# A graph layer on one core: a drain behind every second gather, and 36 instead of 24 groups whose rows all come from TensorE

## The chip, the cores and the metric

The program runs on one core of one Trainium2 chip. The metric is the device time in microseconds of one execution; for the kernel before there are three runs, and one more execution was taken by the hardware profiler. Engines are named as in the profile: PE is TensorE's matmul, PEld its weight load, DVE VectorE, ACT ScalarE, POOL GpSimd, SP SyncE.

## The reference

One layer of a graph network with 6250 nodes of 64 features and 206250 edges, sorted by their target `dst`:

```python
h = jnp.maximum(_layernorm(x, axis=-1), 0.0)
msg = jax.nn.relu(h[src] + edge_attr)
agg = jax.ops.segment_sum(msg, dst, num_segments=x.shape[0])
h = jax.nn.relu((h + agg) @ W1 + b1)
x = x + (h @ W2 + b2)
```

Two steps are hard here: fetching the row `h[src]` for each of the 206250 edges, and summing the messages by target.

## The kernel before, in words

**Groups and sets.** The edges are cut into 268 groups of 768 edges (128 partitions by 6 columns) and a smaller tail group. Groups 0 to 4 are handled in the prologue. The other 264 are bound into 144 *sets* (`GROUPS`, L61 to L63): most sets are two groups, 24 are a single group. Eleven groups make six sets, of which the second is single; six sets make two *chunks* of three.

**Two ways to fetch a row.** For a pair of groups, columns 0 to 2 of each come by GpSimd: one indirect DMA per column (`gather`, L226; the instruction is L229) takes 128 rows of 256 bytes out of `h_rows` in HBM into a slot of the ring `xg`. Columns 3 to 5 come from TensorE. A single group has no gather (`WHOLE`, `pool_cols`, L238): all six of its columns come from TensorE. So each set has six columns of 128 rows from TensorE, and a pair has six gathers besides.

**TensorE's way.** h stands in SBUF as two float16 parts (`hp`). A counting sort, three sets to a chunk and some ten sets ahead (`rank_at` to `sourced`, L327 to L416), gives each edge a place. Then, for two sets at a time, one-hot matrices made by DVE (`found` L564, `backs` L574) select rows by matmul: `across_of` (L586; 8 matmuls L594 at a time) selects, ACT copies the result (L599), `turn_of` (L601; 4 matmuls L604) transposes, ACT copies again (L612), and `pick` (L614; the matmuls L618) puts the rows in the order of the edges. `decode_parts` and `decode_sum` (L683, L684, L690) put the two parts together.

**Messages and sums.** `decode` (L692) adds the picked rows to the edge attributes (DVE, L698, twice a set), and for a pair the gathered rows (DVE, L701, once). ACT takes the relu (`messages`, L708). `window_sum` (L718) sums the messages of a group by 6 matmuls with a one-hot matrix (L722; the one-hot is L655), and DVE adds the window into z (L645). Blocks of 512 nodes that are complete go through the two layers (L748, L758) and out.

**What sets the order.** The order on each engine is that in which the code records the instructions; nothing reorders them. `both_units` (L883) records set k: in each of three steps a turn, an across and two picks, with the decoding of set k-1, the messages and window sums of set k-2 and the counting for sets ahead between them. GpSimd gets its gathers nine sets ahead (`AHEAD`, ring of 11 slots): five times in a set, `pick` calls `fetch_next` (L263), which records one gather of the list `pending` with a manual dependency on the pick's matmul: the gather may start only when that matmul is done. In the prologue the gathers of groups 0 to 20 are recorded in long rows (L1021 to L1034), partly behind matmuls or DVE instructions. DVE's only use of a gathered row is L701. SP issues all other loads.

```python
HEAD = 2 * RG - 1
for g in range(F0, NG + 1, HEAD):
    GROUPS += [(g, g + 1), (g + 2,), (g + 3, g + 4), (g + 5, g + 6), (g + 7, g + 8), (g + 9, g + 10)]
```

`places` (L293) prepares the search for a range of chunks on DVE, in small steps that `searching` (L841) records twice in a set; `stretches` (L284) cuts the columns for it by the pattern of the sets, and `rank_fits` (L366) does so for the slots.

Of the kernel before, what the change touches and what calls it, by code (L numbers as in the profile page):

```python
# [21 lines left out]
G = 6  # L22
GE = P * G
NG = E // GE
# [17 lines left out]
H = 3  # L42
# [13 lines left out]
F0 = 5  # L56
SETS = 3
RG = 2 * SETS
HEAD = 2 * RG - 1
assert (NG + 1 - F0) % HEAD == 0 and SETS == 3  # L60
GROUPS = []  # L61
for g in range(F0, NG + 1, HEAD):
    GROUPS += [(g, g + 1), (g + 2,), (g + 3, g + 4), (g + 5, g + 6), (g + 7, g + 8), (g + 9, g + 10)]  # L63
KS = len(GROUPS)
KD = KS // 2
WHOLE = [gs[0] for gs in GROUPS if len(gs) == 1]
NCH = KS // SETS
# [4 lines left out]
RING, AHEAD, EAS = 11, 9, 4  # L72
# [8 lines left out]
def kernel(  # L81
# [14 lines left out]
    nc = tc.nc  # L96
# [110 lines left out]
    def rows_of(g):  # L207
        if g >= F0:
            return ring(xgs, g)
        if g not in raws:  # L210
            raws[g] = lnp.tile([P, G, D], F32, name="xr", bufs=F0)
        return raws[g]
# [10 lines left out]
    beats, paces = [], []  # L223
    beat = mybir.DependencyInfo(mybir.DependencyClass.Sync, mybir.DependencyReason.ANTI)

    def gather(xg, idx, n, rows, behind=()):  # L226

        for j in range(n):
            it = nc.gpsimd.indirect_dma_start(  # L229
                out=xg[:, j, :], out_offset=None, in_=rows[:, :],  # L230
                in_offset=bass.IndirectOffsetOnAxis(ap=idx[:, j:j + 1], axis=0))
            if j >= n - len(behind):
                tc.add_manual_dep(it.ins, behind[j - n + len(behind)].ins.name, beat, reason="pace")

    def first_col(g):
        return 0 if g < NG else G - CT

    def pool_cols(g):  # L238
        return G if g < F0 else 0 if g in WHOLE else G - H

    def fetch(g, behind=()):
        lo, hi = first_col(g), pool_cols(g)
        if hi:
            gather(rows_of(g)[:, lo:], src_sb[:, g * G + lo:g * G + hi], hi - lo, x if g < RAW else h_rows, behind[lo:])
# [5 lines left out]
    def attr_set(k):  # L250
        gs = GROUPS[k]
        if len(gs) == 2 and gs[1] < NG:
            g = gs[0]
            nc.sync.dma_start(out=eas[(k + RAWS) % EAS].rearrange("p g j d -> p g (j d)"),
                              in_=edge_attr[g * GE:(g + 2) * GE, :].rearrange("(g p j) d -> p g (j d)", g=2, j=G))
        else:
            for g in gs:
                attr_load(ring(eas, g), g)

    pending = [(g, j) for k in range(AHEAD, KS) for g in GROUPS[k] for j in range(first_col(g), pool_cols(g))]  # L260
    assert all(5 * (set_of[g][0] - RING + 1) <= n for n, (g, j) in enumerate(pending))

    def fetch_next(behind):  # L263
        if pending:
            g, j = pending.pop(0)
            gather(rows_of(g)[:, j:], src_sb[:, g * G + j:], 1, h_rows, [behind])

# [15 lines left out]

    def stretches(t_sb, c0, c1):  # L284

        g0 = F0 + c0 // 2 * HEAD
        t = t_sb[:, g0 * G:(g0 + (c1 - c0) // 2 * HEAD) * G].rearrange("p (e g j) -> p e g j", g=HEAD, j=G)
        return ((t[:, :, :2, G - H:], 0, slice(0, 2)),
                (t[:, :, 2:3].rearrange("p e o (g j) -> p e (o g) j", j=H), 0, slice(2, 4)),
                (t[:, :, 3:RG - 1, G - H:], 0, slice(4, RG)),  # L290
                (t[:, :, RG - 1:, G - H:], 1, slice(0, RG)))

    def places(c0, c1):  # L293
        n = c1 - c0
        held = [work.tile([P, WB], F32, name="ow").bitcast(I16) for _ in range(2)]

        def at(i):
            return held[i // 3][:, i % 3 * n * CC:][:, :n * CC].rearrange("p (c s) -> p c s", s=CC)

        own, off, row, second, third = at(0), at(1), at(3), at(4), at(5).bitcast(F16)  # L300
        for src, w, gs in stretches(src_sb, c0, c1):
            nc.vector.tensor_copy(own.rearrange("p c s -> p (c s)")
                                  .rearrange("p (e w g j) -> p e w g j", w=2, g=RG, j=H)[:, :, w, gs], src)
            yield
        nc.vector.tensor_scalar(row, own, 1.0 / RR, 0.5 / RR + 0.5, op0=ALU.mult, op1=ALU.add)
        yield
        nc.vector.scalar_tensor_tensor(off, row, float(-RR), own, op0=ALU.mult, op1=ALU.add)
        yield
        it = nc.vector.tensor_scalar(second, off, 1.0 / PARTS, (RR + 0.5) / PARTS - 0.5, op0=ALU.mult, op1=ALU.add)
        if c0 == 2:  # L310
            paces.append(it)
        yield
        nc.vector.scalar_tensor_tensor(node[:, c0:c1], second, float(PP), row, op0=ALU.mult, op1=ALU.add)
        yield
        nc.vector.tensor_scalar(third, second, float(BB), quarter[:, 0:1], op0=ALU.is_equal, op1=ALU.mult)
        yield
        nc.vector.scalar_tensor_tensor(off, second, float(-PARTS), off, op0=ALU.mult, op1=ALU.add)
        yield
        it = nc.vector.scalar_tensor_tensor(part[:, c0:c1], off, float(RR + BIAS // STEP), third, op0=ALU.add, op1=ALU.add)
        if c0 == 2:  # L320
            paces.append(it)
# [43 lines left out]

    def rank_fits(c):  # L366
        rk = ranks.pop(c).rearrange("p (g j) -> p g j", j=H)
        pieces = ((0, 2, G - H), (2, 4, 0), (4, RG, G - H)) if c % 2 == 0 else ((0, RG, G - H),)
        for u, to, c0 in pieces:
            g = GROUPS[c * SETS + u // 2][0]  # L370
            if c0:
                mine = slot[:, g * G:(g + to - u) * G].rearrange("p (g j) -> p g j", j=G)[:, :, c0:]
            else:
                mine = slot[:, g * G:(g + 1) * G].rearrange("p (g j) -> p g j", j=H)
            nc.vector.scalar_tensor_tensor(mine, rk[:, u:to], float(AMONG + S), mine, op0=ALU.is_lt, op1=ALU.mult)
            yield
# [237 lines left out]
    def pick(k, i, t):  # L614
        d, u = k // 2, k % 2 * 2 + i
        ps = pick_banks[k % 2][i][:, :2 * H * D].rearrange("p (w t d) -> p w t d", w=2, t=H)
        for q in range(Q):
            it = nc.tensor.matmul(ps[:, :, t], backs[d][:, q % QW, q // QW, u * H + t, :],  # L618
                                  picked[d][:, q, u].rearrange("p (w d) -> p w d", w=2), start=(q == 0), stop=(q == Q - 1))
            if (u * H + t) % 2 == q // QW and q % QW == QW - 1 and (u * H + t) % (2 * H) < 2 * H - 1:  # L620
                fetch_next(it)

    def norm_edges(xg):
        s = work.tile([P, G], F32, name="raw_s")
# [183 lines left out]
    searches = []  # L808
# [32 lines left out]
    def searching(u):  # L841
        for c, to in zip(PLACED[2:], PLACED[3:]):
            if u == max(0, 2 * RG * (c // 2) - 60):
                searches.append(places(c, to))
        if searches and next(searches[0], True):
            searches.pop(0)

    def across_at(a):
        if a < KD * Q:
# [31 lines left out]
    behind = []  # L881

    def both_units(k):  # L883
# [11 lines left out]
        for s in range(3):  # L895
# [22 lines left out]
            for t in range(2):  # L918
                pick(k, *divmod(2 * s + t, H))
# [38 lines left out]
    for _ in places(0, 2):  # L958
        pass
# [153 lines left out]
    wide = hot.tile([P, PARTS * BB + J, 4, S], F16, name="found").rearrange("p m u s -> p (m u s)").bitcast(F32)[:, :WB]  # L1113
    with tc.If(any_left > 0):
# [18 lines left out]
        for c in range(NB + 1):  # L1133
            o, xb = result(c, *hidden(c))
# [41 lines left out]
```

## Time and profile before

| what | value |
|---|---|
| median of three runs | 1317.23 us (1314.55 to 1322.07) |
| the profiled execution | 1329.39 us |
| its span, first to last instruction | 1327.7 us |
| mean granted TensorE clock | 0.918 |
| gathers (xg; prologue's xr) | 718; 18 + 12 |
| matmuls | 15593 |
| DMA | 173.72 MB, 131 GB/s on the mean |

Of the page's 40 slices these are the rows of the granted TensorE clock and of the DMA engines' busy share, both in tenths:

```profile
PEclk9767988989999999899998998989889999999898
DMA  5222444444444444444444444444444444444441
```

The first three slices are the prologue, then one steady stage runs to the end. The last gather is issued at 1267.4 us, so in the last 60 us GpSimd has next to nothing to do. A group's row, as they follow in the prediction, reads: line, engine, operation, output and inputs, shapes, count; then busy time in us, mean ns of one; then the idle time of the engine just before them and what ended most of it. "issue" means that the profile shows nothing that was waited for.

### The profile page before, as it was taken

The numbers are of one execution on the slowest core, as the hardware profiler recorded it, in microseconds if no ns is written. First come the engines' busy times: TensorE is split into PE (matmuls) and PEld (weight loads), VectorE is DVE, ScalarE is ACT, GpSimd is POOL, SyncE is SP. The second block draws the span as 40 slices with busy tenths as digits, with TensorE's granted clock in tenths as the row PEclk, the third lists the DMA queues.
The fourth block names the chain that finished last, engine by engine and source line by source line (L and its number), as shares of the span: only waits on it lengthen the run. The fifth ranks groups of instructions, "written<-read, shape, count | busy, mean of one in ns | idle before, by whom it ended". The sixth has DMA issues, their size and how long they took to land. (4 is left out here: it accounts for less than half of the span.)

```text
span 1327.7 us, 39109 instructions
## 1 busy us (share of the span) xinstructions
PE 1041.3 (78%) x15593; PEld 925.0 (70%) x15593; DVE 855.2 (64%) x2167; ACT 853.0 (64%) x1849; POOL 764.3 (58%) x763
## 2 busy tenths in 40 slices
PE   0235888878887887888888888888888887888897
PEld 0224777777776777777777777777777776777796
DVE  8672766666576676576566665665666765766684
ACT  3334666666666666666666666666666666666685
POOL 7674665655565665565565565655566666566510
PEclk9767988989999999899998998989889999999898
DMA  5222444444444444444444444444444444444441
GB/s 187 81 60 93 141 134 128 144 134 122 144 138 135 146 139 134 142 119 134 130 139 140 137 138 127 138 129 139 137 139 141 139 138 141 138 139 141 127 127 55
DMA packets 92790, 173.72 MB, mean 131 GB/s; under 512 B 23673, under 2 KB 61178, under 8 KB 92602
## 3 DMA queue, kind: packets, MB, share of 16 engines
q1 hardware_dynamic: 68554, 146.58, 33.4%
q0 software_dynamic: 23936, 24.56, 9.3%
q8 instruction: 124, 2.03, 0.6%
q14 instruction: 64, 0.52, 0.2%
q10 hardware_dynamic: 112, 0.03, 0.0%
HBM read 167.22 MB, written 3.87 MB: 129 GB/s over the span
## 5 line engine op out<-in xcount | busy, mean ns | idle before, releaser
L229 POOL DMA_INDIRECT xg<-h_rows,src_sb x718 | 730.9, 1018 | 494.1 <-PE pick L618 209.3
L618 PE MATMUL pick<-picked,backs 128*128 128x128 f16 x5184 | 412.2, 230 | 35.3 <-issue 33.8
L618 PEld LDWEIGHTS <-backs 128*128 128x128 f16 x5184 | 329.8, 103 | 61.1 <-issue 50.3
L612 ACT CAST picked<-half 128x512 f16<-128x512 f32 x432 | 249.1, 577 | 177.8 <-remote 53.2
L698 DVE SCALAR_TENSOR_TENSOR ea<-pick,ea 128x192 f32<-128x192 f32 x288 | 101.7, 354 | 401.6 <-PE pick L722 108.1
L599 ACT CAST across<-half 128x512 f16<-128x512 f32 x432 | 253.7, 587 | 158.7 <-PE pick L618 57.4
L594 PE MATMUL half<-found,hp 128*128 128x128 f16 x3456 | 288.4, 229 | 22.9 <-issue 19.9
L594 PEld LDWEIGHTS <-hp 128*128 128x128 f16 x3456 | 233.8, 103 | 39.5 <-issue 31.0
L574 DVE TENSOR_SCALAR backs<-spots,ids 128x1536 f16<-128x1536 int16 x432 | 255.2, 637 | 0.0
L722 PE MATMUL pick<-oh,ea 128*64 128x32 f32 x3176 | 143.2, 226 | 82.1 <-issue 60.2
L722 PEld LDWEIGHTS pick<-oh,ea 128*64 128x64 f32 x3176 | 117.8, 138 | 118.3 <-issue 88.1
L604 PE MATMUL half<-ident_h,across 128*128 128x128 f16 x1728 | 179.4, 229 | 18.0 <-ACT across L599 13.7
L683 ACT CAST both<-pick 128x384 f16<-128x384 f32 x288 | 140.1, 486 | 62.9 <-issue 17.6
L564 DVE TENSOR_SCALAR found<-sources,nodes_of 128x1536 f16<-128x1536 int16 x288 | 170.3, 638 | 9.7 <-issue 9.7
L604 PEld LDWEIGHTS <-across 128*128 128x128 f16 x1728 | 131.0, 103 | 27.2 <-ACT across L599 14.4
L708 ACT ACTIVATE ea<-ea 128x768 f32<-128x768 f32 x144 | 114.5, 795 | 0.7 <-DVE ea L701 0.7
L684 ACT ACTIVATE minus<-both 128x192 f16<-128x192 f16 x288 | 104.5, 363 | 9.1
L655 DVE TENSOR_TENSOR oh<-slot,pick 128x384 f32<-128x384 int16 x144 | 74.0, 514 | 0.3 <-PE pick L690 0.3
L690 PE MATMUL pick<-both,weigh_high 128*128 128x192 f16 x288 | 72.6, 252 | 0.2 <-ACT both L683 0.2
L690 PE MATMUL pick<-minus,weigh_sign 128*128 128x192 f16 x288 | 72.3, 251 | 0.4 <-issue 0.3
L690 PE MATMUL pick<-both,ident_h 128*128 128x192 f16 x288 | 72.5, 252 | 0.0
L690 PE MATMUL pick<-minus,weigh_last 128*128 128x192 f16 x288 | 72.0, 250 | 0.0
(135 smaller groups left out, 809.1 us busy)
## 6 DMA issues: line engine op xcount, KB each, us to landing
sources<-source_row SPq DMA_DIRECT2D x72, 768.0 KB
ea<-in_edge_attr_dram SPq DMA_DIRECT2D x118, 384.0 KB
spots<-spot_rows SPq DMA_DIRECT2D x72, 384.0 KB
xg<-h_rows,src_sb POOLq DMA_INDIRECT x718
ea<-in_edge_attr_dram SPq DMA_DIRECT2D x32, 192.0 KB
xb<-in_x_dram SPq DMA_DIRECT2D x12, 128.0 KB
out_dram<-o SPq DMA_DIRECT2D x12, 128.0 KB
h_rows<-x SPq DMA_DIRECT2D x3, 384.0 KB
```

What stands on the lines that cost most here:

```text
L229: it = nc.gpsimd.indirect_dma_start(out=xg[:, j, :], out_offset=None, in_=rows[:, :], in_offset=bass.IndirectOffsetOnAxis(ap=idx[:, j:j + ...
L564: nc.vector.tensor_scalar(found[d][:, b * PARTS + m:b * PARTS + m + PARTS // 2].rearrange("p m u s -> p (m u s)"), sources[d][:, m * 4 * S ...
L574: nc.vector.tensor_scalar(backs[d][:, q, w].rearrange("p t s -> p (t s)"), spots[d].bitcast(I16), ids[:, w * QW + q:w * QW + q + 1], None, ...
L594: last = nc.tensor.matmul(ps[:, j * P:(j + 1) * P], hp[:, b * PARTS + m].rearrange("p t d -> p (t d)"), found[d][:, b * PARTS + m].rearran ...
L599: nc.scalar.copy(across[d, q].rearrange("p u j s -> p j u s"), ps.rearrange("p (j u s) -> p j u s", j=J, u=4))
L604: last = nc.tensor.matmul(ps[:, u * P:(u + 1) * P], ac[:, u].rearrange("p j s -> p (j s)"), ident_h, start=True, stop=True)
L612: nc.scalar.copy(picked[d][:, q].rearrange("p u d -> p (u d)"), turned.pop((d, q)))
L618: it = nc.tensor.matmul(ps[:, :, t], backs[d][:, q % QW, q // QW, u * H + t, :], picked[d][:, q, u].rearrange("p (w d) -> p w d", w=2), st ...
L683: nc.scalar.copy(both[:, i], picks_of(k, i))
L690: nc.tensor.matmul(picks_of(k, i)[:, 0], weights, rows, start=(j == 0), stop=(j == len(terms) - 1))
L708: nc.scalar.activation(msg, msg, AF.Relu)
L722: last = nc.tensor.matmul(pa[i * D:(i + 1) * D], msg[:, j, :], oh[:, j, :], start=(j < lo + 2), stop=(j >= G - 2))
```

## The change

Two things are changed, and three places follow them.

First, `gather` counts its gathers, and behind every second one it records a drain of GpSimd, an instruction of that engine which has no operands and moves no data. That holds for the prologue's gathers as well.

Second, the pattern of the sets: the first 33 groups keep it (three times six sets with one single set). The other 231 are bound in eleven times twelve sets of 21 groups: six sets as before, then six with two single sets. That makes 150 sets (75 pairs of sets, 50 chunks) of 144, 36 single ones, and 114 pairs with 682 gathers.

What follows: `fetch_next` gets the number of the set and issues at four of its five calls for the sets that lie in a six with two single ones (`RATES`, `gates`); `stretches`, `places` and `rank_fits` know the new pattern; and `searching` records two steps instead of one in its first twelve calls.

```diff
+HEAD, PAIR = 2 * RG - 1, 4 * RG - 3
+SINGLES, DOUBLES = 3, 11
+for h in range(SINGLES + 2 * DOUBLES):
+    last = h >= SINGLES and (h - SINGLES) % 2
+    GROUPS += [(g, g + 1), (g + 2,), (g + 3, g + 4)]
+    g += 5
+    GROUPS += [(g, g + 1), (g + 2,), (g + 3, g + 4)] if last else [(g, g + 1), (g + 2, g + 3), (g + 4, g + 5)]
+    g += 5 if last else 6
+    RATES += [4 if last else 5] * 2 * SETS
...
+            gathers[0] += 1
+            if gathers[0] % 2 == 0:
+                nc.gpsimd.drain()
...
-    def fetch_next(behind):
-        if pending:
+    def fetch_next(k, behind):
+        rate = RATES[min(k + AHEAD, KS - 1)]
+        gates[0] += rate
+        if pending and gates[0] >= 5 * (gates[1] + 1):
+            gates[1] += 1
+            assert k < set_of[pending[0][0]][0] < k + RING
             g, j = pending.pop(0)
             gather(rows_of(g)[:, j:], src_sb[:, g * G + j:], 1, h_rows, [behind])
...
-        pieces = ((0, 2, G - H), (2, 4, 0), (4, RG, G - H)) if c % 2 == 0 else ((0, RG, G - H),)
+        pieces = ((0, 2, G - H), (2, 4, 0), (4, RG, G - H)) if len(GROUPS[c * SETS + 1]) == 1 else ((0, RG, G - H),)
...
-                fetch_next(it)
+                fetch_next(k, it)
...
-        if searches and next(searches[0], True):
-            searches.pop(0)
+        for _ in range(2 if u < 2 * RG else 1):
+            if searches and next(searches[0], True):
+                searches.pop(0)
```

How it moves instructions shows first on DVE, at the decoding of the 41st set, the second of the new single sets. Before (`ea` are the edge attributes, `xg` the gathered rows, `pick` the picked ones, `oh` the one-hot of the window sums):

```order
L574 TENSOR_SCALAR backs<-spots,ids 128x1536
L698 SCALAR_TENSOR_TENSOR ea_145<-pick_195,ea_145 128x192
L698 SCALAR_TENSOR_TENSOR ea_145<-pick_196,ea_145 128x192
L701 SCALAR_TENSOR_TENSOR ea_145<-xg_156,ea_145 128x2x192
L655 TENSOR_TENSOR oh<-slot,pick_195 128x384
L645 ISA
L645 TENSOR_TENSOR z<-z,pick_195 128x32
```

and now:

```order
L600 TENSOR_SCALAR backs<-spots,ids 128x1536
L724 SCALAR_TENSOR_TENSOR ea_145<-pick_204,ea_145 128x192
L724 SCALAR_TENSOR_TENSOR ea_145<-pick_205,ea_145 128x192
L681 TENSOR_TENSOR oh<-slot,pick_204 128x192
L671 ISA
L671 TENSOR_TENSOR z<-z,pick_204 128x32
```

The set has lost its use of gathered rows, and its one-hot is that of one group.

On GpSimd the gathers are listed one ring slot after another, six to a pair of groups (`xg` numbered by the ring of eleven slots; `src_sb` holds the row numbers, `h_rows` is the table in HBM). The drains are not listed in this view. Before, around the 29th set, the first of the new single ones, whose slot is 155:

```order
L229 DMA xg_150<-h_rows,src_sb 128x64 x6
L229 DMA xg_151<-h_rows,src_sb 128x64 x6
L229 DMA xg_153<-h_rows,src_sb 128x64 x6
L229 DMA xg_154<-h_rows,src_sb 128x64 x6
L229 DMA xg_155<-h_rows,src_sb 128x64 x6
L229 DMA xg_156<-h_rows,src_sb 128x64 x6
L229 DMA xg_146<-h_rows,src_sb 128x64 x6
L229 DMA xg_148<-h_rows,src_sb 128x64 x6
```

and now:

```order
L238 DMA xg_150<-h_rows,src_sb 128x64 x6
L238 DMA xg_151<-h_rows,src_sb 128x64 x6
L238 DMA xg_153<-h_rows,src_sb 128x64 x6
L238 DMA xg_154<-h_rows,src_sb 128x64 x6
L238 DMA xg_156<-h_rows,src_sb 128x64 x6
L238 DMA xg_146<-h_rows,src_sb 128x64 x6
L238 DMA xg_148<-h_rows,src_sb 128x64 x6
```

The six gathers into slot 155 are gone; in each row of six that is left, three drains stand, behind the second, fourth and sixth gather. On TensorE the list grows from 24,494 to 25,500 rows, which is 503 weight loads and 503 matmuls more.

More of the change, by code (lines that the diff above doesn't have):

```diff
@@ L58 @@
 RG = 2 * SETS
[L59 to L63, printed above, removed]
+HEAD, PAIR = 2 * RG - 1, 4 * RG - 3
+SINGLES, DOUBLES = 3, 11
+assert F0 + SINGLES * HEAD + DOUBLES * PAIR == NG + 1 and SETS == 3
+GROUPS, RATES = [], []
+g = F0
+for h in range(SINGLES + 2 * DOUBLES):
[5 more added lines that the diff above has]
+    RATES += [4 if last else 5] * 2 * SETS
 KS = len(GROUPS)
@@ L224 @@
     beat = mybir.DependencyInfo(mybir.DependencyClass.Sync, mybir.DependencyReason.ANTI)
+    gathers = [0]
     def gather(xg, idx, n, rows, behind=()):
@@ L260 @@
     pending = [(g, j) for k in range(AHEAD, KS) for g in GROUPS[k] for j in range(first_col(g), pool_cols(g))]
-    assert all(5 * (set_of[g][0] - RING + 1) <= n for n, (g, j) in enumerate(pending))
-    def fetch_next(behind):
-        if pending:
+    gates = [0, 0]
+    def fetch_next(k, behind):
[4 more added lines that the diff above has]
+            assert k < set_of[pending[0][0]][0] < k + RING
             g, j = pending.pop(0)
@@ L284, in stretches @@
     def stretches(t_sb, c0, c1):
[L286 to L291, printed above, removed]
+        wide = c0 >= 2 * SINGLES
+        n, size, chunks = ((c1 - c0) // 4, PAIR, 4) if wide else ((c1 - c0) // 2, HEAD, 2)
+        assert n * chunks == c1 - c0 and (wide or c1 <= 2 * SINGLES)
+        g0 = GROUPS[c0 * SETS][0]
+        t = t_sb[:, g0 * G:(g0 + n * size) * G].rearrange("p (e g j) -> p e g j", g=size, j=G)
+        parts = []
+        for w in range(chunks):
+            a = GROUPS[(c0 + w) * SETS][0] - g0
+            if len(GROUPS[(c0 + w) * SETS + 1]) == 1:
+                parts += [(t[:, :, a:a + 2, G - H:], w, slice(0, 2)),
+                          (t[:, :, a + 2:a + 3].rearrange("p e o (g j) -> p e (o g) j", j=H), w, slice(2, 4)),
+                          (t[:, :, a + 3:a + 5, G - H:], w, slice(4, RG))]
+            else:
+                parts += [(t[:, :, a:a + RG, G - H:], w, slice(0, RG))]
+        return chunks, parts
     def places(c0, c1):
@@ L300, in places @@
         own, off, row, second, third = at(0), at(1), at(3), at(4), at(5).bitcast(F16)
-        for src, w, gs in stretches(src_sb, c0, c1):
+        chunks, parts = stretches(src_sb, c0, c1)
+        for src, w, gs in parts:
             nc.vector.tensor_copy(own.rearrange("p c s -> p (c s)")
-                                  .rearrange("p (e w g j) -> p e w g j", w=2, g=RG, j=H)[:, :, w, gs], src)
+                                  .rearrange("p (e w g j) -> p e w g j", w=chunks, g=RG, j=H)[:, :, w, gs], src)
             yield
```

## The prediction

> **What bounds the kernel now.** I read the busy shares first, then the windows of the stages, then what TensorE and GpSimd waited for, and last the timeline of a few microseconds. The busy shares settle nothing:
>
> ```profile
> PE 1041.3 (78%) x15593; PEld 925.0 (70%) x15593; DVE 855.2 (64%) x2167; ACT 853.0 (64%) x1849; POOL 764.3 (58%) x763
> ```
>
> Nobody is full, TensorE (PE) least idle. The windows say more. The first of these two is the steady stage, the second begins just after the last gather; the columns are PE, weight loads, DVE, ACT, POOL, then the granted clock, DMA share and GB/s.
>
> ```profile
> core 0: us, PE busy (x) PEld busy (x) DVE busy (x) ACT busy (x) POOL busy (x), PEclk, DMA share, GB/s
> 200.00:1200.00 1000.00, 834.74 (x12638) 745.24 (x12639) 649.17 (x1641) 669.34 (x1470) 594.30 (x587) 0.94 0.45 136
> 1268.00:1289.00 21.00, 21.00 (x388) 20.23 (x385) 17.08 (x43) 19.71 (x42) 0.34 (x1) 1.00 0.42 137
> ```
>
> In the steady stage TensorE does 12638/1000 = 12.6 matmuls per us. In the 21 us without gathers it does 388/21 = 18.5, with no idle time and the full clock, at the same 137 GB/s. The sets there still run all their picks, turns and window sums. So a set is not limited by what TensorE computes but by something that ends when the gathers end. At 18.5 per us the 12638 matmuls would have taken 684 us; the other 316 us, over 587 gathers, are **0.54 us lost per gather**.
>
> How it happens is seen in one burst. First GpSimd's timeline, then TensorE's (start, duration, line, in brackets the idle time before it):
>
> ```profile
> 630.77 0.94 POOL L229 DMA_INDIRECT xg<-h_rows,src_sb  x1 [0.30 <-PE pick L690]
> 632.02 0.94 POOL L229 DMA_INDIRECT xg<-h_rows,src_sb  x1 [0.30 <-issue]
> 633.27 0.94 POOL L229 DMA_INDIRECT xg<-h_rows,src_sb  x1 [0.30 <-issue]
> 634.51 0.94 POOL L229 DMA_INDIRECT xg<-h_rows,src_sb  x1 [0.30 <-issue]
> 637.61 1.03 POOL L229 DMA_INDIRECT xg<-h_rows,src_sb  x1 [2.15 <-PE pick L618]
> ```
> ```profile
> 633.45 0.65 PE L722 MATMUL pick<-oh,ea 128*64 128x32 f32 x15 [0.44 <-issue]
> 635.01 0.32 PE L722 MATMUL pick<-oh,ea 128*64 128x32 f32 x4 [0.53 <-issue]
> 636.47 0.43 PE L722 MATMUL pick<-oh,ea 128*64 128x32 f32 x3 [0.54 <-issue]
> 636.83 1.46 PE L618 MATMUL pick<-picked,backs 128*128 128x128 f16 x12
> 1276.03 0.89 PE L722 MATMUL pick<-oh,ea 128*64 128x32 f32 x24
> ```
>
> Gathers stand 0.30 us apart from 630.77 to 635.45. The 24 window sums (L722) begin in it and need from 633.45 to 636.8, against 0.89 us in the last row, where no gather runs. TensorE waits for nothing that the profile names ("issue"), and is released about 1 us after the burst. The prologue has a longer case:
>
> ```profile
> 94.00:101.00 7.00, 3.06 (x27) 2.40 (x25) 6.38 (x16) 1.26 (x3) 5.17 (x7) 0.50 0.48 128
> 101.00:113.00 12.00, 0.16 (x2) 0.00 (x0) 0.00 (x0) 0.00 (x0) 7.15 (x8) 0.50 0.36 127
> ```
>
> For 12 us only GpSimd works there. Joined gathers seem to be what hurts. How many are joined, and how large TensorE's unnamed waits are, stands in the list of waits for 200 to 1200 us:
>
> ```profile
> POOL xg L229 <- PE pick L618: 176.7, 173, 2.8
> POOL xg L229 <- issue: 66.7, 214, 1.7
> PE pick L722 <- issue: 53.1, 97, 1.2
> PE pick L618 <- issue: 29.7, 83, 1.2
> ```
>
> 214 of 587 gathers follow another after 66.7/214 = 0.31 us.
>
> **The change part by part.** The regrouping makes 150 sets of 144. The window sums stay, since the groups stay 268; each new set brings its picks, halves, turns and decoding:
>
> ```profile
> L618 PE MATMUL pick<-picked,backs 128*128 128x128 f16 x5184 | 412.2, 230 | 35.3 <-issue 33.8
> L594 PE MATMUL half<-found,hp 128*128 128x128 f16 x3456 | 288.4, 229 | 22.9 <-issue 19.9
> L604 PE MATMUL half<-ident_h,across 128*128 128x128 f16 x1728 | 179.4, 229 | 18.0 <-ACT across L599 13.7
> L690 PE MATMUL pick<-both,weigh_high 128*128 128x192 f16 x288 | 72.6, 252 | 0.2 <-ACT both L683 0.2
> ```
>
> Over 144 sets these are 36, 24, 12 and, the last row being one of four alike, 8 per set; with half an L589 and two more chunks of 10 counting matmuls that is 6 x 80.5 + 2 x 10 = 503 matmuls. At the pace without gathers they cost 503/18.5 = **+27 us**; at the pace with gathers 503/12.6 = 40 us. I take the first, because the gathers are priced by themselves: 718 become 682, 36 x 0.54 = **-19 us**. These two parts alone are worth +8 us.
>
> ACT gets six sets' copies, DVE six sets' compares and some 18 more casts of the search for places, by these rows 18 x 0.2 us:
>
> ```profile
> L302 DVE CAST ow<-src_sb 128x48 int16<-128x48 int32 (+3 forms) x8 | 1.7, 215 | 0.3 <-issue 0.3
> L612 ACT CAST picked<-half 128x512 f16<-128x512 f32 x432 | 249.1, 577 | 177.8 <-remote 53.2
> ```
>
> Both engines have a third of the steady stage free, so I price that at nothing; ACT is 19.71 of 21 us busy without gathers, so if the pace came near 18.5 matmuls per us, ACT would be next. SP issues three more pairs of source and spot loads, at a DMA share of 0.45, for nothing. The paced gathers fall from 5 a set to 4 in eleven of the 25 chunk pairs; they are issued nine sets ahead, so a late one has some 70 us before DVE adds it (L701).
>
> **The drain.** 341 of them stand behind gathers of xg (and 15 in the prologue behind others). Behind each, the next gather's wait and the gather are queued, and only DVE's L701, nine sets later, waits for those. The trace has no drain after a gather; nearest are GpSimd's own drains, the first after memsets, the others at the program's end:
>
> ```profile
> L1162 POOLq DRAIN  x1: 188/188/188, 0.4 to 0.4; - x1
> L1171 POOLq DRAIN  x3: 40/107/9212, 1301.0 to 1327.4; - x3
> ```
>
> So the duration lies between 0.04 and 9.2 us. I take 0.19 us: it is the drain behind work of GpSimd's own, and the gather's record has ended before it. Can GpSimd afford it? A gather takes
>
> ```profile
> L229 POOL DMA_INDIRECT xg<-h_rows,src_sb x718 | 730.9, 1018 | 494.1 <-PE pick L618 209.3
> 1151.08 3.33 DMA xg<-h_rows,src_sb
> ```
>
> 1.02 us and about 0.30 to the next, so a pair 2.64. Of the 682, 42 are issued in the prologue (14 groups of three), 640 are paced. The picks, which pace the gathers, run now from 120.5 to 1314.3 us:
>
> ```profile
> L618 PE MATMUL pick<-picked,backs x5184: 216/219/314, 120.5 to 1314.3; 128*128 128x128 f16 x200
> ```
>
> If these 1194 us become 1140 (the sum below), a pair has 1140/320 = 3.56 us, and the drain is covered up to **0.9 us**; beyond, GpSimd sets the pace.
>
> What the drain may gain is the loss of the joined gathers. At least nothing; at most everything that gathers cost, 640 x 0.54 = 346 us. Between: 214/587 = 36% of the gathers are joined, a drain behind every second gather stands in half of the joints, 18% of 640 = 117 gathers, and each gets a pause ahead of it in which TensorE can be released. At the mean price that is 117 x 0.54 = **-63 us**. It rests on the burst above, where the release comes after the run of gathers and not within it. The stand of 12 us in the prologue may shrink as well; I count nothing for it.
>
> The sum, on the profiled execution's own 1329.4 us (its span is 1327.7): 1329.4 + 27 - 19 - 63 = 1274 us. The median of the runs shown is 1317.2, 0.991 of the profiled one, so I predict 1274 x 0.991 = **1262 us**.
>
> The clock is part of it: 0.94 in the steady stage, 1.00 without gathers, 0.50 in the prologue's stand. By the Trainium skill (TensorE: Matmul & The Clock Gate, The HAM clock gate) the clock is halved after a window of about 3.4 us in which TensorE is idle; the rows agree in that the slow clock stands where TensorE stood still. By it the clock's share comes back with the stalls and is no further term.
>
> **The rivals.**
>
> *The drain changes nothing for TensorE.* The regrouping remains: 1329.4 + 8 = 1337, or 1325 us. For it: within the burst the drain's 0.19 us is short beside the 1 us that TensorE needs to be released. Against it: where a gather waited for a pick, the pause was 176.7/173 = 1.02 us on the mean, and there TensorE runs.
>
> *The pace without gathers is an accident of the program's end.* Then gathers hold nobody, the new sets cost the mean pace and the 36 gathers give nothing back: 1329.4 + 40 = 1369, or 1357 us, slower. For it: the counting of ranks has ended by 1268 us too. Against it: that is 20 of about 640 matmuls in six sets, while the pace rises by half, and DMA stays at 137 GB/s. The Trainium skill (SBUF — State Buffer, SBUF: two separate sides) says that TensorE's ports never wait on anyone and that only GpSimd and VectorE share one, which speaks for this rival: by it no gather could hold TensorE. The burst and the 12 us do not agree with that, though no row names what is held.
>
> *The drain itself holds TensorE, or GpSimd becomes the bound: slower.* A us of gather costs 0.54/1.02 = 0.53 us. If a drain costs in the same proportion and frees nothing, 341 x 0.19 x 0.53 = 34 us are added: 1371, or 1359 us. If a drain lasts longer than the 0.9 us of cover, GpSimd decides: at 1.2 us a pair takes 3.84, 320 pairs 1229 us where 1194 stood, so 1329 - 1194 + 1229 = 1364 or 1352 us; if it waits for the landing, 3.33 us in the row above, a pair takes 5.97, and 1329 - 1194 + 1910 = 2045, or 2027 us. For it: the 9.2 us drain at the end. Against it: that one follows other instructions of the program's end, 30 us after the last gather. The Trainium skill (PSUM — Partial Sum Buffer, Engine vs sequencer instructions) says that a drain waits for the engine to go fully idle; whether a transfer counts as the engine's, no run here shows.
>
> *More than I count comes back.* If the pauses end half of what gathers cost, 173 us, the sum is 1164, or 1154 us. A long burst is worse than its share, by the prologue; against it, a drain behind every second gather cuts only one or two of the three joints of a burst of four.
>
> **How the numbers follow.** My forecast, with a gain between a third and twice of the 63 us (1305 to 1200), has a chance of 0.50. More than that 0.10. No effect of the drain, 1306 to 1335 us, 0.14. The accident 0.09. The drain as a cost or a bound, 1340 us and more, 0.17. Ten in a hundred lie below 1200, and of the slow cases those of a GpSimd bound, some eight, above 1360: the range is 1200 to 1360; the forecast's own is 1200 to 1305. What a measurement can tell from no change is about 0.5%, so 1310.6 to 1323.8 us: half of the no-effect case and a little of the forecast's edge, 0.09. Faster is 0.50 + 0.10 and a little of the no-effect case, 0.61; slower the rest, 0.30.
>
> **What would show it.** Right: in 200 to 1200 us over 13.3 matmuls per us, fewer gathers that follow another after 0.30 us, "issue" before L722 clearly under 53 us in 1000, the granted clock over 0.94, the drains around 0.2 to 0.6 us and DVE's L701 never waiting for a transfer. The matmuls grow by 503, the xg gathers are 682. Wrong in the drain's gain: the pace at 12.6 with these waits as they are. Wrong in its cost: GpSimd's idle time before a gather ended by nothing but issue, DVE waiting for xg. Wrong in the regrouping's price: no change of the pace, and the end 40 us later. The accident is refuted if the stage behind the last gather again runs at over 18 matmuls per us while the steady pace changes.

## The result, and the profile after

The changed program takes 1824.5 us (median of four, 1819.2 to 1831.5), the program before beside it 1319.7: a ratio of 1.380 with the interval 1.375 to 1.386. The prediction of 1262 us has the wrong sign, and the time lies 465 us above its range.

The windows of the same stretch as before (PE, weight loads, DVE, ACT, POOL, the granted clock, DMA share, GB/s) show every engine less busy, GpSimd too:

```profile
200.00:1200.00 1000.00, 653.14 (x9202) 597.95 (x9200) 476.34 (x1227) 494.26 (x1079) 396.12 (x398) 0.82 0.33 98
```

9.2 matmuls per us instead of 12.6, and 0.40 gathers per us instead of 0.59. Nobody is full because somebody waits, and the list of waits of 200 to 1700 us (total us, times, longest) says for what:

```profile
DVE ea L727 <- DMA xg<-h_rows,src_sb: 649.8, 100, 12.0
ACT picked L638 <- PE half L630: 535.4, 141, 9.6
PEld L644 <- issue: 482.9, 109, 9.1
PE pick L644 <- DVE z L671: 466.2, 91, 9.0
POOL xg L238 <- issue: 261.9, 287, 4.8
```

DVE waits 6.5 us at a time for gathered rows (L727, which was L701). Behind it in DVE's order stands the sum into z (L671), for that waits TensorE, and for TensorE ACT. So one late thing starts the chain: the gathers, which are ordered nine sets ahead. The lines of the drain (duration min/median/max in ns, first and last start), of the gathers and of the picks show the length of the chain:

```profile
L243 POOLq DRAIN  x356: 3126/3690/10583, 3.5 to 1802.1; - x178
L238 POOL DMA_INDIRECT xg<-h_rows,src_sb x682: 942/946/4747, 83.9 to 1803.0; - x171
L644 PE MATMUL pick<-picked,backs x5400: 216/219/314, 117.0 to 1802.8; 128*128 128x128 f16 x193
```

A drain lasts 3.69 us at the median, not 0.19, and the gathers now go on to the last microsecond; before, they ended some 60 us ahead. Three pieces of one cycle show what a drain is made of: GpSimd's timeline, one drain by itself, and the chain of waits at that place.

```profile
640.96 0.99 POOL L238 DMA_INDIRECT xg<-h_rows,src_sb  x1 [2.40 <-DVE ea L727]
642.25 0.95 POOL L238 DMA_INDIRECT xg<-h_rows,src_sb  x1 [0.30 <-issue]
645.54 0.95 POOL L238 DMA_INDIRECT xg<-h_rows,src_sb  x1 [2.34 <-PE pick L644]
```
```profile
L243 POOLq DRAIN  x1: 3496/3496/3496, 636.7 to 636.7; - x1
```
```profile
637.62 2.43 DMA xg<-h_rows,src_sb
640.05 0.03 issue
640.08 0.05 DVEq L727
640.13 0.04 issue
640.18 0.13 DVE ea L727
```

The second gather of the pair begins at 637.62 and its rows have landed at 640.05. The drain began at 636.67, beside the first gather, and lasted 3.50 us: it ends at 640.17, 0.12 us after the landing. So it is with each of the 335 drains after 120 us: from the landing to the drain's end 0.11 to 0.12 us, while the drains themselves differ between 3.1 and 7.2 us. A drain here waits until the rows are there. The next gather begins 0.79 us later, at 640.96; the releasers named in its brackets, DVE and TensorE, are only the last semaphores that were set meanwhile. By the Trainium skill (Perfetto Trace Analysis, DMA Instruction — SWDGE (GPSIMD)) the record of such a gather ends when its descriptors are written and not when the data has moved; the rows agree, with a record of 0.95 us and a landing 2.4 us after its start.

The cycle of a pair adds up: 0.31 us from the first gather to the drain's start, 3.95 the drain on the mean, 0.77 from its end to the next gather, 5.03 in all; 335 pairs are 1685 us, and from the first pick to the last gather are 1803.0 - 117.0 = 1686. GpSimd's chain fills the whole time.

### The profile page after: what moved, and what is told of

It is laid out like the page before. It is cut to its first block, busy times and chain, and to the rows that moved or that the text cites. A ratio compares the mean times of both kernels' runs of the same rounds, so it can differ in the third digit from the quotient of the medians.

```text
span 1818.4 us, 40621 instructions
## 1 busy us (share of the span) xinstructions
PE 1147.5 (63%) x16096; PEld 1045.2 (57%) x16096; DVE 883.1 (49%) x2266; ACT 890.3 (49%) x1923; POOL 716.1 (39%) x727
## 4 chain that ended last, share of the span: by engine, by line
issue 21%; PE 17%; POOLq 10%; POOL 10%; DMA 7%; DVE 2%; DVEq 1%; ACT 0%; ACTq 0%
POOLq L243 10%; POOL xg L238 10%; DMA xg<-h_rows,src_sb 7%; PE pick L644 7%; PE half L620 3%; PE pick L716 2%; PE half L630 2%; PE pick L748 1%; DVE oh L681 1%; DVEq L565 1%; PE half L615 1%; DVE ea L727 0%; PE rows L774 0%; PE rows L784 0%; DVE z L671 0%
## 5 line engine op out<-in xcount | busy, mean ns | idle before, releaser
L238 POOL DMA_INDIRECT xg<-h_rows,src_sb x682 | 682.6, 1001 | 1039.8 <-issue 334.3
L644 PE MATMUL pick<-picked,backs 128*128 128x128 f16 x5400 | 459.6, 245 | 514.4 <-DVE z L671 512.3
L644 PEld LDWEIGHTS <-backs 128*128 128x128 f16 x5400 | 390.2, 111 | 540.8 <-issue 530.8
L727 DVE SCALAR_TENSOR_TENSOR ea<-xg,ea 128x384 f32<-128x384 f32 x114 | 63.6, 558 | 714.3 <-DMA xg<-h_rows,src_sb 714.3
L620 PE MATMUL half<-found,hp 128*128 128x128 f16 x3600 | 312.7, 236 | 2.5 <-issue 1.1
L620 PEld LDWEIGHTS <-hp 128*128 128x128 f16 x3600 | 258.8, 108 | 22.3 <-issue 17.2
L630 PE MATMUL half<-ident_h,across 128*128 128x128 f16 x1800 | 198.5, 239 | 1.5 <-ACT across L625 0.9
L630 PEld LDWEIGHTS <-across 128*128 128x128 f16 x1800 | 148.4, 109 | 5.7 <-ACT across L625 1.4
L748 PE MATMUL pick<-oh,ea 128*64 128x32 f32 x3176 | 123.9, 226 | 6.6 <-ACT ea L734 6.4
L716 PE MATMUL pick<-both,weigh_high 128*128 128x192 f16 x300 | 86.7, 289 | 2.0 <-ACT both L709 2.0
```

The lines of the kernel that those rows point to most:

```text
L238: it = nc.gpsimd.indirect_dma_start(out=xg[:, j, :], out_offset=None, in_=rows[:, :], in_offset=bass.IndirectOffsetOnAxis(ap=idx[:, j:j + ...
L620: last = nc.tensor.matmul(ps[:, j * P:(j + 1) * P], hp[:, b * PARTS + m].rearrange("p t d -> p (t d)"), found[d][:, b * PARTS + m].rearran ...
L630: last = nc.tensor.matmul(ps[:, u * P:(u + 1) * P], ac[:, u].rearrange("p j s -> p (j s)"), ident_h, start=True, stop=True)
L716: nc.tensor.matmul(picks_of(k, i)[:, 0], weights, rows, start=(j == 0), stop=(j == len(terms) - 1))
L748: last = nc.tensor.matmul(pa[i * D:(i + 1) * D], msg[:, j, :], oh[:, j, :], start=(j < lo + 2), stop=(j >= G - 2))
```

## The experiments

Four chips served the runs, and they are of two kinds. On one of them, which served e1 to e4, the program before takes 1006 us (nine runs, without a trace of its own); on the other three it takes 1319.3, 1326.9 and 1320.6 us, as where the prediction was made. Ratios are to the program before on the same chip.

**e1 and e9, the regrouping alone**, on the chip of 1006 us and on one of 1327.

```diff
-            gathers[0] += 1
-            if gathers[0] % 2 == 0:
-                nc.gpsimd.drain()
```

> The changed program without its drains: 36 single sets, 682 gathers, no drain. Landing theory (a drain holds GpSimd until the pair of gathers ahead of it has landed, and that alone costs the 500 us): the whole loss is gone; the regrouping is worth the +8 us of the prediction, so about 1325 us (1305 to 1345), and GpSimd's records are back at 1.25 us from gather to gather in a run. Regrouping theory (the new order of sets, the four gates of five or the 503 matmuls do the harm): it stays above 1600 us. If the prediction's 0.54 us per gather is wrong and a gather costs TensorE nothing, 40 us more than before, 1357 us.

> The changed program without its drains once more; the first time the program before took 1006 us beside it, while the changed program was measured where that takes 1319 us. Where it takes 1319: gathers that hold TensorE (0.54 us each, the prediction's +27 - 19): about 1327 us, within 0.8% of the program before. No such price (the rival of the accident, +40): about 1359 us, 3% over it. Where it takes 1006: 1046 us again. In every case the drains are the rest up to 1819 us.

e1: 1046.1 us, ratio 1.040 (1.038 to 1.041). e9: 1287.3 us, ratio 0.972 (0.966 to 0.977). The loss is gone on both, so it is the drains'. Both times lie below what was expected (1325 to 1357 for e1, 1327 or 1359 for e9). What is left of the change gains 3% on the one kind of chip and costs 4% on the other. Windows of e9 and of e1, the last one behind the last gather of e1:

```profile
200.00:1000.00 800.00, 692.61 (x10973) 623.88 (x10971) 564.17 (x1454) 577.61 (x1288) 468.67 (x465) 0.97 0.47 145
```
```profile
200.00:900.00 700.00, 684.57 (x11779) 636.92 (x11777) 615.79 (x1562) 625.79 (x1384) 509.66 (x504) 1.00 0.60 178
983.00:1003.00 20.00, 20.00 (x369) 19.28 (x368) 16.83 (x43) 18.37 (x39) 0.29 (x1) 1.00 0.45 140
```

13.7 matmuls per us against 16.8. The gathers of e1 follow one another in runs of up to 274 (the prologue's counted) at the same 0.95 us and 0.30 apart, and TensorE is busy for 98% of the time, so they do not hold it. At 16.8 per us the 503 added matmuls are 30 of the 40 us that the regrouping costs there; no run shows where the other 10 come from. And the pace rises to 369/20 = 18.5 behind the last gather on this chip too, so part of that rise belongs to the program's end and not to the gathers.

**e2, the drains alone**, in the program before.

```diff
+            gathers[0] += 1
+            if gathers[0] % 2 == 0:
+                nc.gpsimd.drain()
```

> The program before with a drain behind every second gather, 24 single sets, 718 gathers. Landing theory: 18 pairs of gathers more than in the changed program pass through GpSimd, at 1.25 + 2.84 + 0.12 + 0.77 = 4.98 us each (gather to gather, gather to landing, landing to the drain's end, drain's end to the next gather): 1820 + 18 x 5.0 = about 1910 us (1880 to 1940). TensorE theory (each drain holds TensorE, 500 us over 356 drains = 1.4 us): 374 drains, about 1317 + 525 = 1842 us. Regrouping theory: 1317 us as before.

1951 us, one run. The landing theory is 41 us short: on this chip too a drain ends 0.11 to 0.12 us after the landing, which comes later (2.99 us after the gather's start on the mean, against 2.84). A pair takes 5.15 us, and the 352 pairs with a drain after 120 us make 1813 us, so GpSimd sets the pace here too, beside a program of 1006 us.

**e3 and e8, fewer drains.**

```diff
-            if gathers[0] % 2 == 0:
+            if gathers[0] % 6 == 0:
```

> The changed program with a drain behind every sixth gather. Landing theory: six gathers take 5 x 1.25 + 2.84 + 0.12 + 0.77 = 9.98 us, the 640 paced ones 1065 us, less than the 1194 us that the picks lasted before: GpSimd no longer sets the pace, and the time is that of the regrouping without drains within 40 us (1300 to 1365). TensorE theory: a third of the drains, a third of the loss: about 1325 + 170 = 1490 us.

> The changed program with a drain behind every 24th gather. Landing theory: 24 gathers take 23 x 1.25 + 2.99 + 0.12 + 0.77 = 32.6 us, 1.36 each where they are 1.25 without drains: the 640 paced ones 870 us instead of 800, so 0 to 70 us over the regrouping alone on the same chip (1046 us there), and DVE waits for rows now and then. If each drain costs 1.4 us of TensorE: 28 drains, 40 us over it in any case. No cost at so few drains: within 5 us of it.

e3: 1359.0 us, inside the range, but on the chip where the regrouping alone takes 1046, so for another reason than was given: six gathers take 11.3 us (2.37 to the drain's start, 8.15 the drain, 0.79 after it) instead of 9.98, and GpSimd is the bound still. e8: 1351.7 us, ratio 1.024 (1.021 to 1.027), on a chip of 1319 us. By the ratio of e9 the regrouping alone would take 0.972 x 1319 = 1282 there, so 29 drains cost some 70 us, the upper end of what was expected, but not in the way that was expected: DVE waits for rows for 0.9 us in the whole run, and GpSimd itself waits 253.6 us for picks. After 150 us 304 gathers follow another within 0.40 us of its end, in runs of up to nine, where e9 has 272 in runs of up to five; that longer runs hold TensorE longer would fit, and no run separates it. A drain's record is 3.69 us at the median behind two gathers, 7.87 behind six and 4.93 in e8; it begins while gathers are still queued ahead of it. From the start of the last gather to the drain's end the mean is 2.96 us in the changed program and 4.06 in e3.

**e5 and e6, both programs once more**, on a chip of 1319 us.

> The program before once more, with its own trace on the chip that served the first four runs or another. If that chip again gives 1006 us: TensorE's unnamed waits of the first trace (53 us ahead of the window sums, the 12 us stand in the prologue, 12.6 matmuls per us in the steady stage) are gone although the gathers still follow one another after 0.30 us, and the matmuls come at 17 to 18 per us; then what I called the loss of 0.54 us per gather belongs to the first machine and not to the gathers. If a gather costs TensorE 0.54 us everywhere, the matmuls stay at about 12.6 per us and the time at about 1317 us.

> The changed program itself beside the program before on the same chip. Landing theory: GpSimd's cycle sets the pace and not TensorE, so the time stays near 1824 us (1780 to 1880) whatever the program before takes, and the ratio is about 1.8 where that takes 1006 us. TensorE theory (500 us of loss on top of what TensorE has to do): about 1046 + 500 = 1546 us there.

e5: 1316.6 us, ratio 0.998 (0.996 to 1.001); e6: 1818.9 us, ratio 1.378 (1.376 to 1.381). Since both met a chip of 1319 us, the first part of e5's expectation and e6's ratio of 1.8 stayed untried; e1 shows for the regrouping what e5 was to show, and e2 shows a slow program with drains on the chip of 1006 us.

**e7, two drains instead of one.**

```diff
             if gathers[0] % 2 == 0:
                 nc.gpsimd.drain()
+                nc.gpsimd.drain()
```

> The changed program with two drains behind every second gather. Landing theory: the second finds nothing outstanding, lasts 0.04 to 0.2 us and adds at most 320 x 0.3 = 100 us to the changed program. Fixed-cost theory (a drain lasts its 3.7 us whatever lies ahead of it): 320 x 3.7 = 1180 us more, about 3000 us. TensorE theory: another 500 us, about 2320 us.

1844.9 us in one run, 26 us more than e6. First and second drain:

```profile
L243 POOLq DRAIN  x356: 3079/3641/10654, 3.5 to 1826.9; - x178
L244 POOLq DRAIN  x356: 41/41/177, 12.4 to 1830.3; - x178
```

The second, ahead of which nothing is open any more, lasts 0.04 us. A drain has hardly a price of its own; it costs what it waits for. That ends the fixed cost (3000 us), and a loss of TensorE's for each drain (2320). It cannot tell of a drain that holds TensorE only while it waits; but what TensorE waits for in the changed program is named, DVE and with it the rows.

**e4, e13, e14 and e10, a pause without a wait**: one, three or eight small memsets in place of a drain.

```diff
-                nc.gpsimd.drain()
+                for _ in range(n):
+                    nc.gpsimd.memset(warm, 0.0)
```

> The changed program with a memset of 128x1 by GpSimd in place of each drain: a short pause of GpSimd that waits for no landing. Coupling theory (a pause behind every second gather lets TensorE go, the prediction's -63 us): about 1262 us, and TensorE's unnamed waits ahead of the window sums fall clearly. Rival (so short a pause frees nothing): the time of the regrouping alone, within 10 us. Rival (any instruction between gathers costs GpSimd about what it lasts, and a gather stage at its limit passes that on): up to 340 x 0.3 = 100 us more than the regrouping alone.

> The changed program with one memset of 128x1 in place of each drain, once more, for a chip where the program before takes some 1319 us (the first time it was 1006). Coupling theory (an instruction of GpSimd between two gathers is enough to let TensorE go): 40 to 80 us under the regrouping alone there (0.9715 of the program before), a ratio of 0.91 to 0.94. The memset fits into the 0.30 us between two gathers and changes nothing: 0.9715 within 0.01. Where the program before takes 1006 us: 1.04 again.

> The same with three memsets, 0.3 to 1.0 us. Coupling theory: the pause must be longer than the usual 0.30 us; a ratio of 0.90 to 0.95 where the program before takes some 1319 us. Price theory (every us on GpSimd holds TensorE or fills GpSimd's time): a pair of gathers becomes 0.2 to 0.8 us longer, 320 of them 60 to 250 us, a ratio between 1.02 and 1.15.

> The changed program with eight memsets of 128x1 (0.12 us each in the run with one) in place of each drain: a pause of about 0.7 us beyond the usual 0.30 between two gathers, without a wait for a landing. Coupling theory: where the program before takes 1319 us, TensorE is let go in each pause, 40 to 60 us under the regrouping alone, with less unnamed waiting ahead of the window sums. GpSimd at its limit: where it takes 1006 us, a pair lasts 3.2 us instead of 2.5, 320 pairs 1024 us instead of 800, about 100 to 200 us over the regrouping alone. Nothing: within 10 us of it.

| run | memsets | program before | ratio (interval) |
|---|---|---|---|
| e4 | 1 | 1006 us | 1.040 (1.039 to 1.042), as e1 |
| e13 | 1 | 1321 us | 0.977 (0.973 to 0.981) |
| e14 | 3 | 1321 us | 0.979 (0.974 to 0.985) |
| e10 | 8 | 1327 us | 1.243 (1.235 to 1.250) |

One memset lasts 0.12 us, which lies within the 0.30 us that stand between gathers anyway; it changes nothing (the interval of e9 overlaps). It is no pause, then, and does not test the coupling: 264 gathers after 150 us still follow another within 0.40 us of its end. Three make a real pause, 1.05 us at the median, and no run is longer than two. Waits of 200 to 1000 us, e9 and then e14:

```profile
PE pick L745 <- issue: 32.0, 59, 1.3
PE pick L641 <- issue: 22.3, 62, 1.0
```
```profile
DVE ea L728 <- DMA xg<-h_rows,src_sb: 89.9, 27, 8.2
PE pick L749 <- issue: 6.9, 15, 0.6
PE pick L645 <- issue: 5.7, 19, 0.4
```

TensorE's unnamed waits ahead of the window sums and the picks fall from 54.3 to 12.6 us. Nothing comes of it in time, because GpSimd is at its limit (3.61 us a pair) and DVE waits for rows for 90 us of 800 instead, and TensorE behind it. Eight make GpSimd the bound:

```profile
L244 POOL MEMSET warm<- x2848: 98/98/1105, 6.2 to 1622.5; 128x1 f32 x190
```

Eight memsets last 1.2 to 2.8 us in the timeline of 600 to 620 us, more than the 0.7 expected, and a pair comes to 4.6 us.

**e11 and e12, half of the gathers**, without and with drains. Every second paced gather is left out, so the rows of those columns are stale.

```diff
+    for t in xgs:
+        nc.vector.memset(t, 0.0)
...
             g, j = pending.pop(0)
+            if len(pending) % 2:
+                return
```

> The changed program without drains and without every second of its 640 paced gathers (those columns hold stale rows; the ring is zeroed at the start); TensorE does all that it did. Price of 0.54 us per gather: 320 x 0.54 = 173 us under the regrouping alone where the program before takes 1319 us. Gathers cost TensorE nothing: within 10 us of the regrouping alone. Where the program before takes 1006 us there is little to win: 0 to 40 us.

> The same half of the gathers with a drain behind every second of them: 160 pairs at 4.98 us are 800 us of GpSimd, less than the picks last, so GpSimd does not set the pace. If a drain is harmless as long as GpSimd keeps its lead: within 10 us of the half without drains. If its pause frees TensorE (the prediction's gain, half of 63 us): 20 to 40 us under it where the program before takes 1319 us. If a drain holds TensorE (1.4 us each): 160 x 1.4 = 220 us over it.

e11: 1081.4 us, 206 under e9 on the same chip: 206/320 = 0.64 us for each gather left out, near the 0.54 read from the first trace. But e11 does more than halve the gathers: after 150 us only 15 follow another within 0.40 us of its end, where e9 has 272, and 278 of 308 stand alone. By these joints, as the prediction calls them, the same loss is 206/257 = 0.80 us for each, and no run separates the two. The window sums' rows of e9 and e11 (busy and mean, then idle before) show it, and so does the pace of e11:

```profile
L745 PE MATMUL pick<-oh,ea 128*64 128x32 f32 x3176 | 139.4, 226 | 61.2 <-issue 47.7 <-ACT ea L731 12.5
```
```profile
L749 PE MATMUL pick<-oh,ea 128*64 128x32 f32 x3176 | 121.5, 224 | 4.0 <-issue 2.5 <-ACT ea L735 1.3
```
```profile
200.00:1000.00 800.00, 778.36 (x13364) 722.88 (x13361) 661.78 (x1762) 710.10 (x1569) 294.96 (x283) 1.00 0.54 165
```

16.7 matmuls per us, the pace of e1: on such a chip gathers do hold TensorE, and those that stand alone hold it hardly at all (its unnamed waits ahead of window sums and picks are 2.3 us in these 800). e12: 1170.1 us, 89 above e11. The estimate of 800 us for GpSimd was too low: the landings come later there (3.43 us after the gather's start), a pair takes 0.31 + 4.61 + 0.77 = 5.69 us, and 175 pairs, not 160, fill the 997 us from the first pick to the last gather. So e12 does not tell whether a drain is harmless when GpSimd has time; it never had.

**e15 and e16, pauses in the prologue alone**, with and without the regrouping.

```diff
-            if gathers[0] % 2 == 0:
-                nc.gpsimd.drain()
+            if gathers[0] % 2 == 0 and gathers[0] <= 72:
+                for _ in range(8):
+                    nc.gpsimd.memset(warm, 0.0)
```

> The regrouping without drains, and eight memsets behind every second gather of the prologue alone (36 times). With eight memsets everywhere the first pick stood at 96.6 us instead of 118.7. If the pauses keep TensorE from standing in the prologue: 22 us under the regrouping alone, a ratio of 0.955 where the program before takes some 1319 us. If the later prologue gathers were only pushed behind the first picks and must be paid there: the ratio of the regrouping alone, 0.97. Where the program before takes 1006 us its prologue has no such stand (first pick at 93.5 us): 1.04.

> The program before with these pauses in the prologue alone, 24 single sets and 718 gathers as before. If they end the stand: 1319 - 22 = 1297 us, a ratio of 0.983, and 1.00 where it takes 1006 us. If the gathers are only pushed behind: 1.00 everywhere.

e15: ratio 0.994 (0.990 to 0.997); e16: 1.021 (1.015 to 1.026). Both are slower than was expected for a chip of 1319 us in either case (0.955 or 0.97, and 0.983 or 1.00). The first pick does stand at 96 us, but the postponed gathers follow later in one run of 52, from 157 to 222 us, and there TensorE all but stands (windows of e15):

```profile
137.00:157.00 20.00, 18.25 (x320) 16.92 (x318) 14.55 (x37) 15.80 (x36) 16.08 (x49) 1.00 0.47 137
157.00:177.00 20.00, 8.03 (x82) 4.96 (x80) 4.64 (x15) 4.28 (x11) 15.19 (x17) 0.66 0.37 104
177.00:222.00 45.00, 4.45 (x16) 1.66 (x16) 0.36 (x1) 0.00 (x0) 34.02 (x37) 0.50 0.14 26
```

16 matmuls in 45 us. The stand was not removed but moved, and it became longer. In e16 the longest run after 150 us is 50 gathers.

No run beats both programs on both kinds of chip: the regrouping alone is the best at 1319 us, the program before at 1006.

## Why the prediction was wrong

*The price of the drain.* This step failed: "I take 0.19 us: it is the drain behind work of GpSimd's own, and the gather's record has ended before it." The record's end is not the transfer's end, and the drain waits for the second (0.12 us after the landing, each time; a second drain 0.04 us). The nearest row was the landing, 3.33 us, which was quoted beside it and used for a rival only. The choice went by the kind of instruction; it should have gone by what is unfinished when the drain begins. The Trainium skill (PSUM — Partial Sum Buffer, Engine vs sequencer instructions) says that a drain waits for the engine to go fully idle, and whether a transfer counts had been left open; in these runs a gather's transfer counts.

*The cover.* It says that "the drain is covered up to **0.9 us**; beyond, GpSimd sets the pace", and that is what happened. A pair took 5.03 us, 2.4 more than the 2.64 counted. The step was right and carried the answer as soon as the drain was priced rightly.

*The rival.* The drain that waits for the landing was named with 2027 us. Its mechanism is the one that holds, its size was 11% too high: landing was counted from the end of both gathers and their spacings (2.64 + 3.33 = 5.97 us a pair), but it runs from the start of the second gather, so the pair takes 5.03. With the landing's mean of 2.84 us, 1.25 + 2.84 + 0.12 + 0.77 = 4.98. That it came so near is in part luck: 320 pairs of 5.03 us would have given 1329 - 1194 + 1610 = 1745, or some 1730 us, too little, because 335 pairs and not 320 stood behind the first picks. It shared a chance of 0.17 with two other ways to be slow.

*The pause that lets TensorE go, -63 us.* No run gained it as time. e13's memset is no pause. In e14 TensorE's unnamed waits did fall (12.6 us where e9 has 54.3), perhaps in part because it stood waiting for DVE instead, and the time went to GpSimd's limit. So the release is not refuted and not shown; what the forecast lacked is that a real pause has to be paid on GpSimd. In the changed program these waits are gone as well (idle time before the window sums 6.6 us, nearly all ended by ACT, where before it was 82.1), and it was of no use.

*The price of a gather, 0.54 us.* Its size was in part luck. It took the 18.5 matmuls per us behind the last gather for the pace without gathers, and e1, whose gathers hold nobody, does 16.8 in its steady stage and 18.5 at its end. At 16.8 the price is (1000 - 12638/16.8)/587 = 0.42 us. It is a mean, too, and where it falls was read better in the burst than in the mean: counted over the 1.25 us from the start of a gather, by its place in a run, TensorE did 13.8 matmuls per us at the first, 14.3 at the second, 9.3 at the third and 7.8 at the fourth (the first trace, 200 to 1000 us); in e9 14.7, 14.9, 10.7 and 7.3; in e1 15.2 to 18.6 at every place. What holds TensorE is not shown by any row.

*The regrouping, +8 us.* Measured -38 us in e9 (2.85% of 1326.9) on a chip like the one of the prediction. The matmuls are +503, the gathers 682, as counted. With 0.64 us a gather it would be 27 - 23 = +4 us; another 40 us are not explained by these two terms. In e9 178 of the gathers after 150 us stand alone (over 0.40 us from the one before and the one behind), against 144 before, runs of four and more are fewer (26 against 40), and so are the joints (272 against 325). At 0.80 us a joint that would be 27 - 42 = -15 us, an estimate, and still not all; no run separates it. On the chip of 1006 us the same edit costs 40 us, which is the "accident" rival's number. Its condition, that gathers hold nobody, is true of that chip, but the number is luck: it was worked out at 12.6 matmuls per us, and at that chip's 16.8 it is 30 us.

*What would show it.* The list did point to the right rows: "GpSimd's idle time before a gather ended by nothing but issue, DVE waiting for xg". DVE waits 714 us for xg over the whole run. GpSimd's 261.9 us under issue are only part of the drains' time, as a drain hides behind whatever semaphore was set last.

## What to carry to other kernels

Before an instruction that waits for an engine is placed behind a DMA that the engine issues, ask what is still open at that moment, and price the wait by the landing and not by the record. The work queued behind it then sees one landing per wait: here 5.03 us a pair instead of 2.5, on a queue that had 3.6. And a stall that is read from a trace of one chip may be that chip's: e1 and e9 are the same program and differ by 23% in time, and the same regrouping changes sign between them. A pace that is read from a program's last microseconds is not the pace that its steady stage could have: 18.5 and 16.8 matmuls per us in the same trace.

## What was unexpected about the hardware

In the long run of gathers of e15 TensorE did not stop but went on at one instruction every 1.40 us on the mean, weight load and matmul by turns, while GpSimd issued a gather every 1.25 us:

```profile
192.16 0.27 PE L645 MATMUL pick<-picked,backs 128*128 128x128 f16 x1 [2.54 <-issue]
192.51 0.95 POOL L238 DMA_INDIRECT xg<-h_rows,src_sb  x1 [0.30 <-DMA xg<-h_rows,src_sb]
193.56 0.10 PEld L645 LDWEIGHTS <-backs 128*128 128x128 f16 x1 [2.70 <-issue]
193.77 0.95 POOL L238 DMA_INDIRECT xg<-h_rows,src_sb  x1 [0.31 <-DMA xg<-h_rows,src_sb]
194.96 0.27 PE L645 MATMUL pick<-picked,backs 128*128 128x128 f16 x1 [2.54 <-issue]
195.02 0.95 POOL L238 DMA_INDIRECT xg<-h_rows,src_sb  x1 [0.30 <-DMA xg<-h_rows,src_sb]
196.36 0.10 PEld L717 LDWEIGHTS <-weigh_high 128*128 128x128 f16 x1 [2.70 <-issue]
```

192.16, 193.56, 194.96, 196.36: even steps, with nothing that the profile names as the cause. It looks like the stall of the first trace, seen long enough to show a rate. On the chip of 1006 us runs of up to 274 gathers leave no such mark (e1, 16.8 matmuls per us). What in the chips makes the difference stays open.
